# Moving column differences and a residual add to GpSimd, pacing the light work at 0.6, and spacing the scan weights' transfers, in a two-layer image kernel

## The chip, the cores and the metric

The kernel runs on one core of a Trainium2 chip. The metric is the time on the device in microseconds (us): 6881.47 us is the median of three runs (6868.02 to 6881.63). One further execution was taken with the hardware profiler: it took 6861.66 us, and its span from first to last instruction is 6859.9 us. All durations of single instructions come from that execution.

Six actors matter. TensorE (PE) multiplies matrices. VectorE (DVE), ScalarE (ACT) and GpSimd (POOL) do elementwise work. SyncE (SP) only issues transfers (DMA). The DMA engines carry them. Each engine works through its own queue in order: an instruction that waits holds everything behind it on that engine.

## The reference

Four images `x[b]`, each of 96 channels of 128 x 128, pass through two layers with a residual around each. Cut to what matters:

```python
# layer 0: a state-space block on the group-normalised image
z  = silu(dwconv3x3(einsum("bchw,dc->bdhw", gn(x), in_w) + in_b) + dw_b)   # 192 channels
xs = [z by rows, z by columns, both reversed]                              # 4 directions k
dts, B, C = split(einsum("bkdl,ked->bkel", xs, x_proj_weight))
delta = softplus(einsum("bkrl,kdr->bkdl", dts, dt_projs_weight) + bias)    # "scan weights"
h  = scan over l of h = exp(delta * A) * h + delta * B * xs;  y = h * C + Ds * xs
yn = layernorm(sum of the 4 directions) * ln_w + ln_b
x  = x + einsum("bdhw,cd->bchw", yn, out_w) + out_b          # residual of layer 0

# layer 1: on the group-normalised result
xr, x1, x2 = relu_split_norm(gn(x))       # two maps, one for x > 0 and one for x <= 0
key, qry, value = conv3x3(x1, aw1), conv3x3(x2, aw2), conv3x3(x1, aw3)
w_attn = softmax(key patches @ qry patches)                  # a 3x3 kernel per image
y1 = layer_norm(conv3x3(value, w_attn))
y2 = layer_norm(conv3x3(x2, w_conv2)) * x1
x  = x + xr + w_full @ concat(y1, y2) + b_full
```

## The kernel before

The program works in stages, and in most of them two streams of work are woven together. Each stream is a Python generator that emits instructions and yields a cost. `co_run(left, right, pace)` takes a step of `left`, adds its cost times `pace` to a debt, and lets `right` emit until the debt is paid. A larger `pace` therefore lets `right` end sooner beside `left`. The images are numbered 0 to 3.

**Set-up and projection.** `project` makes `z` strip by strip: matmuls on PE (L613), a tanh on ACT (L488), a product on DVE (L489). Beside image 0 it also gathers the statistics of images 1 and 2: `image_stats` loads tiles `xst` from GpSimd's queue (L401), two in flight, and DVE takes their statistics (L404). `other_weights` prepares weights that only the scan and the norm need later. It splits the `dt` weights in three pieces and puts them in place with 54 transfers `wdt` (L246) and 12 transfers `wbc` (L249), all issued by GpSimd. They are emitted in one piece, when the first strips of image 0 have been projected.

**Scan.** `ssm_scan` runs beside the projections of images 1 to 3, beside the norm of image 0, and beside the convolutions of image 0 (`direct_maps`). Each step uses ACT, GpSimd (two products and sums of 128 x 1024, L813 and L846) and DVE (the scan itself, L834).

**Norm.** `Image.norm` is `ssm_output`, then `split_norm`. `ssm_output` works on 16 chunks of 1024 columns. A chunk goes through three rounds of the loop, as `new`, `mid` and `old`. In the last of them `scaled` multiplies the projection by the inverse deviation `r` (L992), adds bias and the residual tile `xr` (L993), and takes statistics (L994), all on DVE and twice for a chunk. The inverse deviations go out to memory and come back spread over the channels, by two transfers on GpSimd's queue (L970, L978); the second waits until the first has landed. `split_norm` has two passes of 16 chunks: the first counts and squares (L1078, L1081, L1085); the second writes the two maps `x1d` and `x2d`. For each chunk and map of the second pass GpSimd clears a column (L1159), ACT scales (L1161), DVE masks (L1166), and SP stores `half`. There are two buffers for each map's `half`.

**Attention of one image.** `attention` has two parts. In the *large convolutions* (`pair_sets`, not for image 0, whose part is `direct_maps`) the weights `wd` convolve `x1d` and `x2d`, and the taps of the softmax are gathered. `Taps.weights` then makes the image's own 3 x 3 weights `wa`. In the *short convolution* these convolve the map `vd`, in 22 chunks of six rows. Both parts use a transform along the columns: `columns` makes from three tiles of rows `y` the tiles `t` that PE multiplies. For the first two tiles there are a difference of 128 x 768 (L1265), a sum (L1266) and a difference (L1267) of 128 x 384; the third is made on DVE (L1272, L1274). The second tile's are always on GpSimd. The first tile's are on the engine `first`: GpSimd in the large convolutions, DVE in the short one. `products` multiplies (L1289, L1300) into four PSUM banks, and `outputs` empties them: ACT copies one (L1338), DVE combines (L1330 to L1333), and DVE takes statistics (L1598 in the short convolution).

**Last stage of one image.** `Image.close` (`attn_output`) mixes the results and writes the output in 16 chunks (L1737 to L1751).

The main loop at the end of the kernel weaves these: beside `attend(b)` runs `close(b - 1)`, and behind it `norm` of image `b + 1`, at a pace of 1.5 for b = 0 and 0.5 afterwards.

```python
        left = imgs[b].attend(psl)
        co_run(left, light, 0.5 if b else 1.5)
        drain(left)
        drain(light)
```

For the part from the set-up to the end of the scan, `in_order` ties each engine's instructions to the order in which they were emitted. After that (from the norm of image 1 on) a scheduler may reorder them.

Of the kernel before, what the change touches and what calls it, by code (L numbers as in the profile page):

```python
# [11 lines left out]
AF = mybir.ActivationFunctionType  # L12
ALU = mybir.AluOpType
# [49 lines left out]
def kernel(  # L63
# [26 lines left out]
    nc = tc.nc  # L90
# [122 lines left out]
    def other_weights():  # L213

        wdt = const.tile([128, 3, NK, 128], BF16, name="wdt", tag="wdt")
        wbc = const.tile([128, 3, 2, 128], BF16, name="wbc", tag="wbc")
        outws = const.tile([C, 2, C], F32, name="outws", tag="outws")  # L220
        outbs = const.tile([C, 1], F32, name="outbs", tag="outbs")
        with (
            tc.tile_pool(name="w0", bufs=1, side="right") as w0,
            tc.tile_pool(name="ps0", bufs=1, space=PSUM, side="right") as ps0,
        ):
            wf = w0.tile([RANK, NK, 2 * C], F32, name="wf")
            nc.gpsimd.dma_start(wf, dt_wT)
            outw = w0.tile([C, 2, C], F32, name="outw")
            nc.sync.dma_start(outw, out_wT)
            one = w0.tile([3, 128], BF16, name="one")  # L230
            nc.vector.memset(one, 1.0)
            nc.vector.memset(wdt, 0.0)
            nc.vector.memset(wbc, 0.0)
            yield
            flat = "p k c -> p (k c)"
            pieces = split3(w0, wf.rearrange(flat), [RANK, NK * 2 * C])
            for row, ch, g, p, n in (
                (row, *part)
                for img, *part in PARTS
                for row in ((KI * img,) if part[1] == 1 else (0, 64))  # L240
            ):
                for w in range(3):
                    src = pieces[w].rearrange("p (k c) -> p k c", k=NK)[:, :, ch : ch + n]
                    for i in range(3):
                        at = row + w * 18 + i * RANK
                        nc.gpsimd.dma_start(wdt[at : at + RANK, g, :, p : p + n], src)  # L246
                for q in range(2):
                    at = row + 54 + q
                    nc.gpsimd.dma_start(wbc[at : at + 5 : 2, g, q, p : p + n], one[:, :n])  # L249
            for j in range(2):  # L250
                nc.vector.tensor_scalar(
                    outws[:, j], outw[:, j], lnw[:, j : j + 1], None, ALU.mult
                )
            pb = ps0.tile([C, 1], F32, name="pb")
            for j in range(2):
                nc.tensor.matmul(
                    pb, lhsT=outw[:, j], rhs=lnb[:, j : j + 1], start=(j == 0), stop=(j == 1)
                )
            nc.vector.tensor_add(outbs, pb, outb)

            pw = ps0.tile([C, C], F32, name="pw")
            for j in range(2):
                nc.tensor.matmul(
                    pw, lhsT=mean192, rhs=outws[:, j], start=(j == 0), stop=(j == 1)
                )
            nc.vector.tensor_sub(outws, outws, pw.unsqueeze(1).to_broadcast([C, 2, C]))
        yield wdt, wbc, outws, outbs
# [647 lines left out]
    def ssm_output(b, yms, xnew, stats, ps, side):  # L915
# [5 lines left out]
        with tc.tile_pool(name="c2", bufs=2, side=side) as p2:  # L921
# [3 lines left out]
            ys, sums_of, near, made = {}, {}, {}, {}  # L925
# [49 lines left out]
            def spread_out(c):  # L975
                xr, to = near[c]
                r = p2.tile([C, SN], F32, name="r")
                nc.gpsimd.dma_start(r, to.partition_broadcast(C))  # L978
                near[c] = xr, r
# [10 lines left out]
            def scaled(c, h, po):  # L990
                xr, r = (t[:, bass.ts(h, CH)] for t in near[c])
                nc.vector.tensor_mul(r, po, r)  # L992
                nc.vector.scalar_tensor_tensor(xr, r, outbs, xr, ALU.add, ALU.add)  # L993
                nc.vector.bn_stats(stats[:, 2 * c + h], xr)  # L994

            for c in range(3):
# [2 lines left out]
            for c in range(NS + 2):  # L999
                new, old = c < NS, c - 2 if c >= 2 else None  # L1000
                mid = c - 1 if 1 <= c <= NS else None
                if old is not None:
                    po = projected(old, 0)
                yield 1.2
                if new:
                    squares(c)
                if mid is not None:
                    inverse(mid)
                    roots(mid)
                if old is not None:  # L1010
                    scaled(old, 0, po)
                    po = projected(old, 1)
                    ys.pop(old)
                if mid is not None:
                    back(mid)
                yield 1.4
                if new:
                    sums(c, 0)
                if mid is not None:
                    spread_out(mid)  # L1020
                yield 1.4
                if old is not None:
                    scaled(old, 1, po)
                    load_y(c + 1)
                if new:
                    sums(c, 1)
                yield 1.4
                if old is not None:
                    nc.sync.dma_start(xnew[:, bass.ts(old, SN)], near.pop(old)[0])
                yield 1.4  # L1030
                if new:
                    rows(c)
                yield 1.4
# [220 lines left out]
    def columns(pool, tiles, r, first):  # L1254

        def of(t, k, p0=0, p1=128):
            v = t[p0:p1, k : k + r * PW].rearrange("p (h w) -> p h w", w=PW)
            return v[:, :, 0:W].rearrange("p h (j e) -> p e h j", e=2)

        made = []  # L1260
        for i, eng in ((0, first), (1, nc.gpsimd)):
            y = tiles[i]
            t = pool.tile([128, 4, CR * W // 2], F32, name=f"t{i}", tag=f"t{i}")
            v = t[:, :, : r * W // 2].rearrange("p i (h j) -> p i h j", h=r)
            eng.tensor_sub(v[:, 0:2], of(y, 0), of(y, 2))  # L1265
            eng.tensor_add(v[:, 2], of(y, 0)[:, 1], of(y, 2)[:, 0])  # L1266
            eng.tensor_sub(v[:, 3], of(y, 2)[:, 0], of(y, 0)[:, 1])  # L1267
            made.append(t)
        y = tiles[2]
        t = pool.tile([128, CR * W // 2], F32, name="t2", tag="t2")  # L1270
        v = t[:, : r * W // 2].rearrange("p (h j) -> p h j", h=r)
        nc.vector.tensor_sub(v[0:64], of(y, 0, 0, 64)[:, 0], of(y, 2, 0, 64)[:, 0])  # L1272
        x = of(y, 0, 64, 128)
        nc.vector.scalar_tensor_tensor(  # L1274
            v[64:128], x[:, 0], signs[64:128], x[:, 1], ALU.mult, ALU.add
        )
        made.append(t)
        return made
# [535 lines left out]
    with tc.tile_pool(name="wp", bufs=1, side="left") as wp:  # L1814
        stats = {}
        stats[0], run = image_stats(0, wp)
        weights = project_weights(wp)
        with tc.tile_pool(name="a0", bufs=8, side="right") as p2:
            drain(run(p2, 8, nc.sync))
        first = len(traced())  # L1820
        others = other_weights()
        for images, pace in (([0], 0.25), ([1], 0.75), ([2, 3], 1.35)):
            left = projections(images, weights, stats, wp, psl)
            if images[0] == 0:
                next(left)
                next(others)
                made = pair_weights()
                next(made)
                while ready[0] < 2:
                    next(left)  # L1830
                maps = [
                    [new_map(f"{n}{i}") for n in ("x1d", "x2d", "vd")] for i in range(2)
                ]
                four, nine = next(made)
                wdt, wbc, outws, outbs = next(others)
            co_run(left, last, pace)
            drain(left)
    istats = [ctx.enter_context(tc.tile_pool(name="istats0", bufs=1, side="left"))]
    imgs = {0: Image(0)}
    left = imgs[0].norm(yms[0][0], psl, "left")  # L1840
    co_run(left, last, 0.5)
    drain(left)
    left = direct_maps(imgs[0], psl)
# [22 lines left out]
    for b in range(NB):  # L1866
        light = []
        if b:
            light.append(imgs[b - 1].close(psr, "right"))
        if b + 1 == 1:  # L1870
            light.append(next_norm)
        elif b + 1 < NB:
            imgs[b + 1] = Image(b + 1)
            light.append(imgs[b + 1].norm(yms[(b + 1) // 2][(b + 1) % 2], psr, "right"))
        light = chain(*light)
        left = imgs[b].attend(psl)
        co_run(left, light, 0.5 if b else 1.5)
        drain(left)
        drain(light)
    drain(imgs[NB - 1].close(psr, "right"))  # L1880
# [75 lines left out]
```

## Time and profile before

| part of the profiled execution | from, us | to, us | length, us |
|---|---|---|---|
| projections (PE, L613) | 49.9 | 2079.2 | 2029.3 |
| norm of image 0, up to its last map | 2131.3 | 2530.8 | 399.5 |
| `direct_maps` of image 0 | 2545.0 | 3567.2 | 1022.2 |
| short convolution of image 0 | 3618.4 | 3816.3 | 197.9 |
| large convolutions of image 1 | 3829.7 | 4598.2 | 768.5 |
| short convolution of image 1 | 4626.6 | 4866.5 | 239.9 |
| large convolutions of image 2 | 4884.3 | 5659.3 | 775.0 |
| short convolution of image 2 | 5687.3 | 5924.6 | 237.3 |
| large convolutions of image 3 | 5943.9 | 6549.3 | 605.4 |
| short convolution of image 3 | 6577.6 | 6736.0 | 158.4 |
| last stage of image 3 | 6750.2 | 6854.6 | 104.4 |

The rows are the times of the first and last matmuls of each part (of the mask L1166 for the norm). A busy share over the whole span (PE 82%, DVE 74%, GpSimd 51%, ACT 42%) averages over parts with different limits, so each part is read on its own. In the views below, a row of the table of stretches gives the window, its length, and for each engine the busy time with the number of instructions in brackets, then the granted clock of PE, the share of the DMA engines in use and the rate in GB/s. A row of the table of waits gives the waiting engine and line, what it waited for, the total in us, how many times, and the longest. A row of the timeline gives start, duration, engine, line, operation, tiles and shapes; a bracket at its end is the idle time ahead of it and what ended it.

### The profile page before, as it was taken

How to read it: one execution, taken by the hardware profiler on the slowest of the kernel's cores; microseconds unless marked ns; L12 is line 12 of the kernel's file. 1: busy time of each engine (PE TensorE's matmuls, PEld its weight loads, DVE VectorE, ACT ScalarE, POOL GpSimd, SP SyncE). 2: the span in 40 equal slices, each digit the busy share in tenths (PEclk: the TensorE clock that was granted, in tenths of full speed). 3: DMA queues.
4: the chain of work that ended last, by engine and by line, in shares of the span. 5: the costliest groups of instructions: out<-in, count | busy, mean ns of one | idle time of the engine just before them, and what ended most of it. 6: DMA issues, size and time to landing. Idle time of an engine off the chain costs nothing. (4 is left out here: it accounts for less than half of the span.)

```text
span 6859.9 us, 74337 instructions
## 1 busy us (share of the span) xinstructions
PE 5650.5 (82%) x22236; PEld 2322.2 (34%) x22236; DVE 5060.8 (74%) x6916; ACT 2912.9 (42%) x3685; POOL 3478.8 (51%) x2264
## 2 busy tenths in 40 slices
PE   5889978978886539899977898887798886788987
PEld 2333323322221114444432343343343342334432
DVE  3247779979897779898458767678766778775688
ACT  1257768777875567676241122132112132121112
POOL 2236759879794339788104434334433434444641
PEclk9999989989996659999988899998899998899998
DMA  6666777866766676766767666567565667565556
GB/s 167 151 160 182 193 214 200 229 165 179 219 176 182 182 205 191 216 174 194 195 186 216 167 166 155 155 170 216 157 176 147 163 163 203 163 173 138 140 155 178
DMA packets 796460, 1227.58 MB, mean 179 GB/s; under 512 B 218750, under 2 KB 558726, under 8 KB 783580
## 3 DMA queue, kind: packets, MB, share of 16 engines
q1 hardware_dynamic: 778572, 1183.90, 63.4%
q0 software_dynamic: 16208, 38.42, 2.0%
q8 instruction: 178, 2.92, 0.2%
q14 instruction: 222, 1.82, 0.1%
q10 hardware_dynamic: 1280, 0.53, 0.0%
HBM read 858.12 MB, written 296.46 MB: 168 GB/s over the span
## 5 line engine op out<-in xcount | busy, mean ns | idle before, releaser
L613 PE MATMUL bank<-y,wp 128*128 128x512 f32 (+3 forms) x3584 | 1317.0, 626 | 94.2 <-DVE z L489 38.6
L1289 PE MATMUL bank<-t,wd 128*128 128x384 f32 (+2 forms) x4224 | 1145.5, 496 | 78.3 <-DVE s L1331 20.6
L1265 POOL TENSOR_TENSOR t<-y 128x768 f32<-128x768 f32 (+1 forms) x352 | 565.4, 1607 | 1257.2 <-PE bank L1289 391.4
L846 POOL TENSOR_TENSOR y<-y,dl 128x1024 f32<-128x1024 f32 x384 | 1051.4, 2738 | 258.6 <-DVE dl L838 228.3
L813 POOL TENSOR_TENSOR dl<-dl,u 128x1024 f32<-128x1024 f32 x384 | 1004.4, 2616 | 249.7 <-ACT dA L789 122.4
L834 DVE TENSOR_TENSOR_SCAN dA<-dA,pBC 128x512 f32<-128x512 f32 x768 | 981.4, 1278 | 30.9
L1338 ACT COPY s<-bank 128x384 f32<-128x384 f32 (+2 forms) x292 | 135.9, 465 | 1900.0 <-PE bank L1300 1837.5
L1289 PEld LDWEIGHTS bank<-t,wd 128*128 128x128 f32 (+1 forms) x4224 | 557.2, 170 | 622.0 <-issue 323.4
L727 PE MATMUL pBC<-xr,wbc 60*128 60x512 bf16 (+1 forms) x1536 | 459.9, 403 | 349.6 <-DVE dA L834 276.2
L838 DVE TENSOR_TENSOR dl<-dA,pBC 128x512 f32<-128x512 f32 x768 | 528.1, 688 | 272.3 <-PE pBC L727 199.8
L1289 PE MATMUL bank<-t,wa 128*96 128x384 f32 (+1 forms) x1408 | 561.3, 548 | 202.8 <-DVE t L1266 128.7
L613 PEld LDWEIGHTS bank<-y,wp 128*128 128x128 f32 (+3 forms) x3584 | 459.1, 169 | 764.9 <-issue 661.2
L1647 PE MATMUL bank<-y,wn 128*128 128x384 f32 (+5 forms) x2408 | 670.2, 505 | 38.4 <-ACT ring L1661 16.1
L656 ACT ACTIVATE dl<-pd,dtb 128x512 f32<-128x512 f32 x768 | 486.3, 684 | 172.0 <-PE pd L727 163.8
L817 DVE TENSOR_TENSOR pBC<-dl,pBC 128x512 f32<-128x512 f32 x768 | 527.5, 687 | 4.7 <-POOL dl L813 3.8
L1330 DVE TENSOR_TENSOR d<-s,bank 128x384 f32<-128x384 f32 (+2 forms) x292 | 155.8, 534 | 486.1 <-ACT s L1338 435.8
L789 ACT ACTIVATE dA<-dl,negA 128x1024 f32<-128x1024 f32 x384 | 420.3, 1141 | 2.3
L1647 PEld LDWEIGHTS bank<-y,wn 128*128 128x128 f32 (+3 forms) x2408 | 306.2, 167 | 335.2 <-issue 165.9
L1289 PEld LDWEIGHTS bank<-t,wa 128*96 128x96 f32 x1408 | 241.0, 184 | 507.9 <-issue 305.6
L1266 POOL TENSOR_TENSOR t<-y 128x384 f32<-128x384 f32 (+1 forms) x352 | 382.2, 1086 | 0.0
L727 PEld LDWEIGHTS <-wbc 60*128 60x128 bf16 (+1 forms) x1536 | 103.5, 96 | 781.7 <-issue 767.6
L656 ACT ACT_TABLE_LOAD x245 | 314.3, 1283 | 109.0 <-PE pd L727 102.3
(257 smaller groups left out, 7965.0 us busy)
## 6 DMA issues: line engine op xcount, KB each, us to landing
u<-zb SPq DMA_DIRECT2D x192, 1024.0 KB
yms<-y SPq DMA_DIRECT2D x96, 512.0 KB
y<-yms SPq DMA_DIRECT2D x64, 768.0 KB
xn<-xnew SPq DMA_DIRECT2D x128, 384.0 KB
y<-y SPq DMA_DIRECT2D x128, 258.2 KB
zb<-z SPq DMA_DIRECT2D x64, 512.0 KB
y<-vd SPq DMA_DIRECT2D x168, 193.8 KB
y<-in_x SPq DMA_DIRECT2D x56, 480.0 KB
```

What stands on the lines that cost most here:

```text
L613: nc.tensor.matmul(blocks(pz[p:e]), lhsT=ws[k][:, d, c : c + e - p], rhs=window(ys[k], at, d, n), start=(i == 0), stop=(i == len(terms) - 1),)
L656: nc.scalar.activation(dst, src, AF.Softplus, bias=bias)
L727: nc.tensor.matmul(p, lhsT=w[rows], rhs=xr[rows, at : at + CH], start=True, stop=True)
L789: nc.scalar.activation(live[m]["dA"], live[m]["dl"], AF.Exp, scale=negA[:, g % 3, k : k + 1])
L813: nc.gpsimd.tensor_mul(t, t, u_view(n))
L817: nc.vector.tensor_mul(p, live[n]["dl"][:, bass.ts(half, CH)], p)
L834: nc.vector.tensor_tensor_scan(h, h, p, init, ALU.mult, ALU.add)
L838: nc.vector.tensor_mul(live[n]["dl"][:, sl], live[n]["dA"][:, sl], live[n]["C", half])
L846: nc.gpsimd.tensor_add(v, v, t.rearrange("p (a b) -> p a b", b=W))
L1265: eng.tensor_sub(v[:, 0:2], of(y, 0), of(y, 2))
L1289: nc.tensor.matmul(pc[p:e, :n], lhsT=w[:, i, c : c + e - p], rhs=t[k][:, i, :n], start=(k == 0), stop=False,)
L1647: nc.tensor.matmul(pc[p:e, :n].rearrange("p (h w) -> p h w", w=W), lhsT=w[:, c : c + e - p], rhs=v[:, :, 0:W], start=(i == 0), stop=(i == ...
```

## The change

```diff
@@ other_weights @@
                 for w in range(3):
+                    yield
                     src = pieces[w].rearrange("p (k c) -> p k c", k=NK)[:, :, ch : ch + n]
...
@@ main part, after pair_weights @@
-                wdt, wbc, outws, outbs = next(others)
+                got = next(others)
+                while not got:
+                    next(left)
+                    got = next(others)
+                wdt, wbc, outws, outbs = got
...
@@ ssm_output: scaled @@
                 nc.vector.tensor_mul(r, po, r)
-                nc.vector.scalar_tensor_tensor(xr, r, outbs, xr, ALU.add, ALU.add)
+                nc.gpsimd.tensor_add(xr, r, xr)
                 nc.vector.bn_stats(stats[:, 2 * c + h], xr)
...
                 if mid is not None:
+                    xr = near[mid][0]
+                    nc.scalar.activation(xr, xr, AF.Identity, bias=outbs)
                     spread_out(mid)
...
@@ columns @@
             eng.tensor_sub(v[:, 0:2], of(y, 0), of(y, 2))
-            eng.tensor_add(v[:, 2], of(y, 0)[:, 1], of(y, 2)[:, 0])
-            eng.tensor_sub(v[:, 3], of(y, 2)[:, 0], of(y, 0)[:, 1])
+            nc.gpsimd.tensor_add(v[:, 2], of(y, 0)[:, 1], of(y, 2)[:, 0])
+            nc.gpsimd.tensor_sub(v[:, 3], of(y, 2)[:, 0], of(y, 0)[:, 1])
...
@@ main loop @@
-        co_run(left, light, 0.5 if b else 1.5)
+        co_run(left, light, 0.6 if b else 1.5)
```

Four things change.

- **Scan weights.** The 54 `wdt` transfers come in 18 groups of three. Between two groups one step of the projection is emitted.
- **Residual.** The bias goes into the loaded residual tile on ACT, one instruction of 96 x 1024 for a chunk. The sum of 96 x 512 moves from DVE to GpSimd, twice for a chunk. The statistics stay on DVE and now read what GpSimd wrote.
- **Columns.** In the short convolution, the sum and the small difference of the first tile move from DVE to GpSimd. In the large convolutions they were there already.
- **Pace.** Beside the attention of images 1 to 3, the light work is emitted at a pace of 0.6 instead of 0.5.

## The prediction on record

> **What bounds the kernel now.** The chain that ended last covers only the final stage, so I read the table of stretches first, cut at the borders of the parts.
>
> ```profile
> 4160.00:4558.00 398.00, 361.00 (x1712) 162.99 (x1709) 283.38 (x403) 72.83 (x118) 159.87 (x173) 0.94 0.60 160
> ...
> 4627.00:4884.00 257.00, 192.82 (x550) 80.68 (x549) 213.72 (x316) 50.02 (x61) 109.49 (x93) 0.81 0.71 200
> ...
> 6577.00:6736.00 159.00, 145.54 (x526) 61.68 (x528) 144.03 (x222) 11.00 (x23) 77.33 (x57) 0.98 0.60 168
> ```
>
> The first row is the large convolutions of image 1 beside the norm: PE is busy 361 of 398 us (91%), DVE 71%. The second is the short convolution of image 1 beside the norm's second pass, the third that of image 3 with nothing beside it. The same work takes 240 us there and 158 us here; alone it fills PE and DVE alike (146 and 144 of 159 us). Next, the waits in the short convolution of image 1:
>
> ```profile
> POOL t L1265 <- DMA y<-vd: 69.8, 16, 8.1
> ...
> PE bank L1289 <- DVE t L1266: 52.5, 15, 4.5
> ```
>
> PE waits 15 times for the first tile, which DVE makes from behind the masks of the second pass. PE's granted clock falls to 0.81 there, so its matmuls stretch as well (193 us busy against 146). Third, the timelines of GpSimd, DVE and PE around the scan weights:
>
> ```profile
> 183.84 4.95 POOL L246 DMA_DIRECT2D wdt<-piece  x9
> 188.78 1.08 POOL L249 DMA_DIRECT2D wbc<-one  x2
> 189.85 1.07 POOL L401 DMA_DIRECT2D xst<-in_x  x2
> ```
>
> ```profile
> 192.78 0.69 DVE L404 BATCH_NORM_STATS2 stats<-xst 96x6 f32<-96x512 f32 x1 [40.94 <-DMA xst<-in_x]
> ```
>
> ```profile
> 194.11 7.66 PE L613 MATMUL bank<-y,wp 128*64 128x512 f32 x28 [31.17 <-DVE z L489]
> ```
>
> The tile `xst` is queued on GpSimd behind all the weights' transfers. DVE stands 40.9 us in front of it, the product `z` is behind it on DVE, and PE stands 31.2 us. Fourth, the residual in image 0's norm (DVE, then GpSimd):
>
> ```profile
> 2203.09 0.62 DVE L992 TENSOR_TENSOR r<-bank,r 96x512 f32<-96x512 f32 x1
> 2203.74 0.75 DVE L993 SCALAR_TENSOR_TENSOR xr<-r,outbs,xr 96x512 f32<-96x512 f32 x1
> 2204.53 0.69 DVE L994 BATCH_NORM_STATS2 xstats<-xr 96x6 f32<-96x512 f32 x1
> ```
>
> ```profile
> 2203.46 0.55 POOL L970 DMA_DIRECT2D rd<-mq  x1 [3.96 <-DVE mq L968]
> 2205.54 0.52 POOL L978 DMA_DIRECT2D r<-rd  x1 [1.53 <-DMA rd<-mq]
> 2206.07 2.37 POOL L813 TENSOR_TENSOR dl<-dl,u 128x1024 f32<-128x1024 f32 x1
> ```
>
> DVE does it back to back, while GpSimd is held by a transfer that waits for another.
>
> **What the Trainium skill says.** "GPSIMD Engine Reference", section 3.1, gives an fp32 add of 2048 elements as 4497 ns on GpSimd and 2293 on DVE, 1.96 times. Here the sum L1266 averages 1086 ns on GpSimd and 968 on DVE; both means hold interference, and the measured ones are used. Section 8 of that page says that the two share SBUF interfaces and contend when DVE reads two SBUF inputs. The trace agrees: beside GpSimd's columns one residual (L993) took 6689 ns, where the median is 747. "DMA: Bandwidth & Descriptors", section on the anatomy of one DMA, puts about 2 us of fixed cost on a transfer, mostly completion; the 1.53 us hold at L978 fits. "Perfetto Trace Analysis", on the most-contended engine, calls matmul busy time a bad measure; the 193 against 146 us for the same matmuls agrees, so I compare lengths of parts.
>
> **The change part by part**, against the span of 6859.9 us.
>
> *Scan weights.* The transfers stay: 54 x 560 + 12 x 546 ns = 36.8 us of GpSimd. In the changed program's order, single `xst` loads now stand between groups of 3 to 11 of them, and one load more stands ahead. Behind the gap DVE takes one `xst` every 5.8 us (203.88, 209.70 in the timeline); nine such steps are 52 us, room for 36.8 + 9 x 0.51 = 41.4 us of issues. A group of 11 holds a load by 6 us, and with two buffers a load has about 11.6 us. So nearly all of PE's 31.2 us goes; I leave 4 for the first group: **-27** (-31 to -10). The projection is one chain on PE here and the scan has not begun, so it passes to the end. The added projection steps come before `co_run` starts and only shift emission: 0.
>
> *Pace.* In the changed order on DVE, all 32 masks of the norm stand ahead of the short convolution's first evacuation, 14 of them ahead of the softmax's maximum and 18 behind; in the kernel before most stood between the short convolution's chunks. So the short convolutions of images 1 and 2 should take image 3's time: (239.9 - 158.4) + (237.3 - 158.4) = **-160** (-162 to -130). The masks must go somewhere. Behind the softmax's maximum there are 9 pairs. In image 0, where they also stand together, SP's stores of `x1d` begin at 3572.11, 3577.28, 3582.64 and 3588.58: 5.5 us a pair, since two buffers wait for the stores. 9 x 5.5 = 49 us to the first evacuation, where image 1 now has 25 (maximum 4609.2, evacuation after the first products, 4634.5): +24 for each image, **+48** (+10 to +80). Ahead of the maximum, 7 pairs at 5.5 are 38 us beside some 55 us of large convolution, in which DVE gets 55 x 0.59 (its share alone in image 3) + 14 x 1.58 = 55 us, so full: I take 10 us for each image, **+20** (0 to +60). The loads of rows for PE are behind these stores on SP, which waits for the masks; that is in the upper bound. The rest of the light work only moves closer together; PE has the same work at the same 91%: 0.
>
> *Columns.* 88 sums and 88 differences leave DVE (85.2 + 81.2 us) for GpSimd, 22 chunks for each image. GpSimd then has per chunk 1.69 + 4 x 1.23 = 6.6 us in image 3 (its own rows there), DVE 144 - 34 = 110 us of 159. PE works 6.6 us a chunk and has 7.2. GpSimd is a chunk ahead and also waits for `vd`, so it just fits: image 3 0 (-8 to +15), and images 1 and 2 are priced by it above. In image 0, whose masks stay in the short convolution, PE waited 27 us for L1266, but GpSimd also sits there behind column clears that wait for stores (37 us): **-10** (-25 to 0).
>
> *Residual.* DVE loses 128 x 1.17 = 149 us, off the path where PE is at 91%. ACT gains 64 instructions, 1.24 us each by L1161 (same shape, same operation), with ACT 18% busy: hidden, and the residual's load has been issued well before. GpSimd gains 128 adds of 1.2 us (half of L813's 2.37; bounds 0.8 to 2.7): hidden by 60% idle time in the large convolutions. But the statistics now wait for GpSimd. In image 0 the order is as written: the first half costs 1.2 instead of 0.75, the second is behind the spread transfer: from the end of L992 at 2203.71 to 2206.06 + 1.2 is 3.5 us instead of 0.8. That is 3.2 us for each chunk, and up to 2.4 more with a scan product in front. Behind those statistics stand the reciprocal and the scan. DVE waits 39 us there for `mq` and `r` (2.4 a chunk), which will take up most: 16 x 1 = **+15** (-5 to +50). In the norms of images 1 to 3 the scheduler puts other DVE work (some 8 us by its rows) between product and statistics: 0 (-10 to +130).
>
> Sum: -27 - 160 + 48 + 20 - 10 + 15 = -114, a span of 6746, -1.66%. The unprofiled median is 6881.47: 6881.5 x 0.9834 = **6767**.
>
> **The rivals.** *(A) More.* The masks cost nothing in the large convolutions and the gap: -160 - 27 - 10 = -197, that is 6684. For it: DMA is at 0.60 there. Against it: 5.5 us a pair was measured.
>
> *(B) Only moved.* The second pass costs the large convolutions what it cost the short ones, 80 us an image instead of 34: -114 + 92 = -22, 6859. For it: the pairs in a row are bound by their stores. Against it: most of the 80 us was a tangle of DVE's order and GpSimd's clears, which goes.
>
> *(C) Slower: the statistics' wait takes DVE.* An add stands behind a group of columns on GpSimd (1.45 + 0.84 + 0.82 = 3.1 us) and behind the spread transfer; DVE stops at the statistics, the evacuations behind it stop, PE runs out of banks. If each chunk loses 3.1 + 2.4 = 5.5 us in images 0, 2 and 3 that is 48 x 5.5 = 264 us: -114 - 15 + 264 = +135, 7017. It decides from 129 / 48 = 2.7 us a chunk. For it: in the stretch of the first row GpSimd waits 114.7 us for DVE's `mq` and 54.1 us for PE. Against it: the order leaves 8 us.
>
> That the change doesn't do what it says is excluded by the order of its instructions.
>
> **Chances.** Forecast 0.55, A 0.15, B 0.16, C 0.14. Its own bounds added in squares are about 50 us each way (6717 to 6817); the range reaches up to B and a mild C, and down towards A: 6700 to 6885. About 0.2% (14 us) is what a measurement tells from no change. Faster: 0.55 + 0.15 + most of B (0.11) = 0.81; same 0.04; slower 0.15.
>
> **What would show it.** Right: PE's 31 us gap at 160 gone; short convolutions of images 1 and 2 at 155 to 165 us with PE waiting little for `t`; the gap behind the softmax some 24 us longer; statistics' waits on GpSimd near 3 us a chunk in image 0, near none later. Wrong: short convolutions above 190 us with PE waiting for GpSimd's `t`; large convolutions above 830 us; DVE idle ahead of the statistics by over 130 us in all.

## The result and the profile after

The changed kernel takes 6773.61 us (median of four runs, 6767.27 to 6776.06) against 6881.55 us for the kernel before (four runs). The ratio is **0.9846**, interval 0.9829 to 0.9864: 108 us or 1.5% faster. The forecast was 6767 us. In the profiled execution the span went from 6859.9 to 6772.8 us, 87 us less.

By the medians the total came out near the forecast, but partly by luck. Beside the later run of the same code the kernel before took 6864.5 us and the changed one 6771.6, 93 us less (ratio 0.9862, interval 0.9844 to 0.9879, which leaves the forecast's 0.9834 just outside), and the two profiles are 87 and 89 us shorter than that of before, where the prediction's sum was 114. This table sets the terms of the prediction's sum against the two profiles taken of the changed kernel (the second belongs to a later run of the same code and shows how far such lengths repeat). All figures are differences to the profile of before, in us, from the first and last matmuls of each part; the ends of gaps are those of the neighbouring parts. A gap is the stretch between the last matmul of the large convolutions and the first of the short one. Rows of a few us (the last stage of image 3 among them) are left out, so the second sum differs from its span by 3.

| part | predicted | changed kernel | again |
|---|---|---|---|
| set-up and projections | -27 | -23 | -28 |
| norm of image 0, its 16 output projections | +15 | +18 | +18 |
| from there to the end of `direct_maps` | 0 | +3 | +9 |
| short convolution of image 0 | -10 | -11 | -14 |
| short convolutions of images 1 and 2 | -160 | -176 | -176 |
| gaps ahead of these two | +48 | +59 | +58 |
| large convolutions of images 1 and 2 | +20 | +42 | +40 |
| large convolutions of image 3 | 0 | +17 | +17 |
| gap and short convolution of image 3 | 0 | -16 | -16 |
| sum | -114 | -87 | -92 |

First the table of stretches after (length, then busy time and instructions of PE, PEld, DVE, ACT and GpSimd, granted clock, DMA share, GB/s): the large convolutions and the short convolution of image 1, and the short convolution of image 3.

```profile
3819.00:4616.00 797.00, 685.12 (x3099) 318.98 (x3097) 512.34 (x761) 213.61 (x309) 347.06 (x335) 0.92 0.62 165
4673.90:4824.60 150.70, 150.05 (x528) 63.85 (x528) 126.83 (x191) 14.27 (x26) 106.51 (x97) 0.99 0.73 207
...
6503.40:6647.90 144.50, 142.44 (x528) 62.47 (x528) 117.90 (x184) 11.34 (x23) 109.64 (x95) 0.99 0.66 184
```

The short convolution of image 1 went from 240 to 151 us. PE is busy for all of it, at a granted clock of 0.99 instead of 0.81, and DVE has only 127 us of work there, instead of 214 in the 257 us of the prediction's row. For the large convolutions, the row of the whole part in the kernel before is this:

```profile
3829.70:4598.20 768.50, 684.24 (x3090) 312.70 (x3094) 526.89 (x742) 170.33 (x259) 294.86 (x295) 0.94 0.62 163
```

PE has the same work (685 and 684 us) and the part is 28 us longer: what was packed in there beside it was not free (ACT, for one, was busy 214 us instead of 170). The waits around the short convolution of image 1 after (window 4600 to 4690):

```profile
PE bank L1293 <- DMA wa<-watd: 41.1, 1, 41.1
POOL half L1163 <- DMA x1d<-half: 30.7, 7, 12.2
```

The 15 waits of PE for the first tile (52.5 us before) are gone. Ahead of the part there is now one wait of 41.1 us, for the weights `wa`. GpSimd meanwhile waits 30.7 us, and ACT 20.1, for buffers of the masked maps, whose stores are under way.

The set-up after, DVE and then PE:

```profile
185.49 0.69 DVE L406 BATCH_NORM_STATS2 stats<-xst 96x6 f32<-96x512 f32 x1 [6.58 <-DMA xst<-in_x]
```

```profile
168.79 7.93 PE L615 MATMUL bank<-y,wp 128*64 128x512 f32 x28 [10.42 <-DVE z L491]
```

DVE's one wait of 40.9 us for `xst` has become several, of which this one, 6.6 us, is the longest. PE's 31.2 us in front of the projection have become 10.4. What is left is another wait: the product `z` that PE waits for stood 14.3 us for ACT's `z` on DVE, not for `xst`; in the kernel before no such wait was over 4.9 us.

Last, DVE's waits in the norm of image 0 (window 2110 to 2355):

```profile
DVE xstats L996 <- POOL xr L995: 99.2, 30, 9.7
DVE mq L960 <- DMA mq<-st: 15.2, 3, 13.1
```

The statistics wait 30 times for GpSimd's sum, 3.3 us each time, which is 6.2 us for each of the 16 chunks. For comparison the kernel before had waits for `r` and `mq` (window 2131 to 2358):

```profile
DVE r L992 <- DMA r<-rd: 19.0, 6, 5.0
DVE mq L958 <- DMA mq<-st: 15.5, 6, 6.3
```

### The profile page after: what moved, and what is told of

Read it like the earlier page. It is cut to its first block, busy times and chain, and to the rows that moved or that the text cites. A ratio compares the mean times of both kernels' runs of the same rounds, so it can differ in the third digit from the quotient of the medians.

```text
span 6772.8 us, 74661 instructions
## 1 busy us (share of the span) xinstructions
PE 5600.1 (83%) x22236; PEld 2315.3 (34%) x22236; DVE 4783.9 (71%) x6612; ACT 2984.4 (44%) x3749; POOL 3789.6 (56%) x2568
## 3 DMA queue, kind: packets, MB, share of 16 engines
q14 instruction: 224, 1.84, 0.1%
## 5 line engine op out<-in xcount | busy, mean ns | idle before, releaser
L1293 PE MATMUL bank<-t,wd 128*128 128x384 f32 (+2 forms) x4224 | 1162.7, 503 | 62.1 <-ACT s L1342 21.6
L1293 PEld LDWEIGHTS bank<-t,wd 128*128 128x128 f32 (+1 forms) x4224 | 575.2, 173 | 602.1 <-issue 340.7
L1293 PE MATMUL bank<-t,wa 128*96 128x384 f32 (+1 forms) x1408 | 496.8, 500 | 148.1 <-DMA wa<-watd 125.2
L1270 POOL TENSOR_TENSOR t<-y 128x384 f32<-128x384 f32 (+1 forms) x440 | 454.1, 1032 | 127.7 <-DMA y<-vd 82.8
L1271 POOL TENSOR_TENSOR t<-y 128x384 f32<-128x384 f32 (+1 forms) x440 | 432.7, 984 | 0.0
L1293 PEld LDWEIGHTS bank<-t,wa 128*96 128x96 f32 x1408 | 220.5, 168 | 415.0 <-issue 228.6
```

What stands on the lines that cost most here:

```text
L1270: nc.gpsimd.tensor_add(v[:, 2], of(y, 0)[:, 1], of(y, 2)[:, 0])
L1293: nc.tensor.matmul(pc[p:e, :n], lhsT=w[:, i, c : c + e - p], rhs=t[k][:, i, :n], start=(k == 0), stop=False,)
```

## The experiments

The theory at this point was the prediction's: four edits, each worth its term. The rivals were that the gains come from another edit than the one I credited, that a gain is given back later, or that the residual costs more (rival C) or less than its term. All ratios below are to the kernel before, run beside the kernel in question.

### One edit alone, four times

**Scan weights alone.** The edit is the first two pieces of the diff.

```diff
                 for w in range(3):
+                    yield
...
-                wdt, wbc, outws, outbs = next(others)
+                got = next(others)
+                while not got:
+                    next(left)
+                    got = next(others)
```

> The kernel before with the scan weights' transfers spread out alone. My theory: PE's gap of 31 us in the projection of image 0 shrinks to under 10, and the 23 to 27 us gained there reach the end: ratio 0.9960 to 0.9967. Rival (given back): the stretch up to the end of direct_maps is bound by the scan, which does not start earlier, so the end of direct_maps stays at 3567 us and the ratio is within 0.9985 to 1.0015.

Measured: 0.9956 (0.9941 to 0.9970), span 6833.0 us, 27 less than before. The projections end at 2051.9 instead of 2079.2 us and `direct_maps` at 3541.8 instead of 3567.2. Two waits of PE for `z` are left in the set-up, 11.1 us together, as in the changed kernel (11.0). What is won in front of the scan is still there at its end and at the end of the program, so it was not given back.

**Columns alone.**

```diff
-            eng.tensor_add(v[:, 2], of(y, 0)[:, 1], of(y, 2)[:, 0])
-            eng.tensor_sub(v[:, 3], of(y, 2)[:, 0], of(y, 0)[:, 1])
+            nc.gpsimd.tensor_add(v[:, 2], of(y, 0)[:, 1], of(y, 2)[:, 0])
+            nc.gpsimd.tensor_sub(v[:, 3], of(y, 2)[:, 0], of(y, 0)[:, 1])
```

> The kernel before with the two column operations on GpSimd alone; the norm's second pass still lies beside the short convolutions of images 1 and 2. My theory: 10 us less in image 0; in images 1 and 2 the wait of PE for the first tile (52 and 49 us) mostly goes, since GpSimd makes it without standing behind the masks, so the short convolutions fall from 240 to about 200 us: in all 70 to 100 us less, ratio 0.985 to 0.990. Rival (tangle): those waits pass to GpSimd's column clears and to vd's loads behind the stores of the maps, the short convolutions stay above 230 us, and the ratio is 0.996 to 1.000.

Measured: **0.9826** (0.9808 to 0.9844), the largest of the four and more than I expected; the medians differ by 122 us, the spans by 126. The short convolution of image 1, its row of the table of stretches, and its waits:

```profile
4614.50:4809.60 195.10, 163.47 (x529) 68.12 (x529) 181.09 (x248) 47.48 (x57) 133.06 (x123) 0.92 0.84 241
```

```profile
PE bank L1300 <- DVE t L1274: 29.1, 14, 3.4
```

It takes 195 us instead of 240 (image 2: 197 instead of 238), with the masks still beside it (ACT's and DVE's instruction counts show them: 57 and 248 against 26 and 191 in the changed kernel). PE no longer waits for the first tile; it waits 29 us for the third, which DVE makes. The gap ahead is 25 us and the large convolutions have not grown. Images 0 and 3, beside whose short convolutions the pace changes nothing, give 14 us each. Half of what I had credited to the pace comes from the columns alone, and without its price.

**Residual alone.**

```diff
-                nc.vector.scalar_tensor_tensor(xr, r, outbs, xr, ALU.add, ALU.add)
+                nc.gpsimd.tensor_add(xr, r, xr)
...
+                    xr = near[mid][0]
+                    nc.scalar.activation(xr, xr, AF.Identity, bias=outbs)
```

> The kernel before with the residual's sum on GpSimd and the bias on ACT alone. My theory: 15 to 20 us more in the norm of image 0, where DVE's statistics stand waiting for GpSimd, and nothing in the other images: ratio 1.0022 to 1.0030. Rival C (the statistics' wait takes DVE in all norms): 130 us or more, ratio above 1.015. Rival (relief): the 149 us taken from DVE shorten the large convolutions of images 1 and 2, ratio below 0.998.

Measured: 1.0043 (1.0028 to 1.0057), a loss of 27 us by the medians and 30 by the ratio, about twice the term. DVE's waits in the norm of image 0 of this kernel:

```profile
DVE xstats L994 <- POOL xr L993: 96.5, 30, 9.1
```

This is the wait of the changed kernel, 3.2 us each time, and the part is 18 us longer. `direct_maps`, beside which the norm of image 1 runs with the same wait (51.1 us, 30 times, by its table of waits), is 14 us longer. Two profiles of one kernel differ by up to 7 us in that part, so all fourteen profiles of this document have to be taken together. The norm of image 0 lasts 244 to 245 us in the six profiles that have the residual's sum on GpSimd with the statistics right behind it, and 220 to 227 in the seven that have it on DVE: 22 us more by the means. `direct_maps` lasts 1026 to 1036 us in the seven profiles with the sum on GpSimd and 1022 to 1030 in the other seven: 7 us more. The two places together are the size of the loss. Rival C asked for 264 us; nothing of that size is there.

**Pace alone.**

```diff
-        co_run(left, light, 0.5 if b else 1.5)
+        co_run(left, light, 0.6 if b else 1.5)
```

> The kernel before with the pace of 0.6 alone. My theory: the short convolutions of images 1 and 2 fall from 240 and 237 us to 158, as image 3's, 160 us less; the gap behind the softmax and the last part of the large convolutions take 70 to 100 us of it back: 60 to 92 us less in all, ratio 0.9866 to 0.9913. Rival (columns did it): without the columns on GpSimd the short convolutions stay above 200 us and the ratio is above 0.996.

Measured: 0.9952 (0.9939 to 0.9964), span 26 us less. The short convolution of image 1:

```profile
4692.90:4852.70 159.80, 152.43 (x528) 63.42 (x528) 148.86 (x229) 14.29 (x26) 77.75 (x59) 0.98 0.69 195
```

It does become as short as image 3's, 160 us, and image 2's too: 158 us won, as the prediction said. But the gaps grow by 58 us, the large convolutions of images 1 and 2 by 65 and those of image 3 by 15. Of the 158 us, 138 go back, where I had expected 70 to 100.

### Two edits on the same wait

**The changed kernel without the residual,** then **without the columns.** Each puts the lines of the kernel before back at that place.

> The changed kernel with the residual's sum back on DVE in one instruction. Theory 1 (the residual costs what it cost alone, in the norm of image 0 and beside direct_maps): about 20 to 35 us less than the changed kernel, ratio to the kernel before 0.980 to 0.982. Theory 2 (with the norm packed closer at 0.6, relief of DVE in the large convolutions pays for it): no gain, ratio 0.984 to 0.986.

Measured: 0.9832 (0.9814 to 0.9849), span 6747.9 us, 25 less than with the residual; the medians differ by 20 to 22 us. That lies between the two theories. The residual is likely a loss in this company too (the intervals of the two ratios overlap), somewhat smaller than alone.

> The changed kernel with the short convolution's two column operations back on DVE. Theory 1 (pace and columns overlap: either of them clears the short convolutions of images 1 and 2): it loses what the columns bring when no mask is beside them, 9 us for each of images 1 and 2, 14 for image 3, 11 for image 0, about 43 us: ratio 0.990 to 0.992. Theory 2 (their gains add): it loses 126 us, ratio 1.001 to 1.004.

Measured: 0.9925 (0.9909 to 0.9941). Against the changed kernel (0.9846, and 0.9862 in the run below) the columns are worth 0.6 to 0.8% beside the pace, where they are worth 1.74% alone. Four edits alone add up to -0.44 - 1.74 + 0.43 - 0.48 = -2.2%; together they give -1.4 to -1.5%. The missing part is what columns and pace both take from the same place, the short convolutions of images 1 and 2: 86 and 158 us alone, but 176 together.

**Scan weights and columns without pace and residual.**

> The kernel before with the scan weights and the columns alone: neither residual nor pace. Theory 1 (with the columns on GpSimd, the pace of 0.6 takes more from the large convolutions and the gap than it gives, and the residual is a loss): 150 to 155 us less than before, ratio 0.977 to 0.979, ahead of the changed kernel by some 45 us. Theory 2 (pace is needed): ratio 0.984 or more.

Measured: **0.9784** (0.9769 to 0.9800), median 6726.1 us, faster than the changed kernel. The kernel without the residual, which ran with it, differs from it by the pace alone: 0.9832 against 0.9784. So with the columns in place, a pace of 0.6 is not a gain but a loss of 0.4 to 0.5% (25 us between the medians, and the intervals do not overlap). By the parts of the two profiles it takes 99 us from the short convolutions of images 1 and 2 and adds 60 to the gaps and 59 to the large convolutions.

**The changed kernel once more,** beside the runs with a third buffer and with later statistics:

> The changed kernel itself, unedited, as the measure for the three beside it: 0.983 to 0.986 of the kernel before.

Measured: 0.9862 (0.9844 to 0.9879), median 6771.59 us, in agreement with the first measurement. Its parts are in the table at the top.

### Where the gap comes from

In the gap ahead of the short convolution of image 1 in the changed kernel, the timelines of SP (SPq is its queue), of DVE and of PE:

```profile
4644.10 0.37 SPq L1174 DMA_DIRECT2D x1d<-half  x1
...
4662.85 0.37 SPq L1174 DMA_DIRECT2D x1d<-half  x1
...
4663.74 1.41 SPq L1467 DMA_DIRECT2D watd<-ring  x1
...
4670.29 0.30 SPq L1235 DMA_DIRECT2D wa<-watd  x1
```

```profile
4636.80 0.82 DVE L1198 SCALAR_TENSOR_TENSOR ring<-ring 96x288 f32<-96x288 f32 x2
```

```profile
4631.08 1.68 PE L1462 MATMUL bank<-ident,sm 96*96 96x96 f32 x9 [4.76 <-DVE sm L1456]
4673.86 7.34 PE L1293 MATMUL bank<-t,wa 128*96 128x384 f32 x16 [41.10 <-DMA wa<-watd]
```

And in the kernel before, DVE and SP at the same place:

```profile
4618.85 0.82 DVE L1194 SCALAR_TENSOR_TENSOR ring<-ring 96x288 f32<-96x288 f32 x2
```

```profile
4619.70 0.30 SPq L1463 DMA_DIRECT2D watd<-ring  x1
```

PE has transposed the softmax at 4632.8 us, and DVE has made the weights from it at 4637.6, 21 us behind the last large convolution, as in the kernel before. There their way to memory (`watd`, L1463) is issued at once. Here it is issued only at 4663.74, 26 us later, because SP works in order and 33 other transfers stand ahead of it: 16 loads of rows `y` for the short convolution, 5 stores of the large convolutions' results, and, of the norm's second pass, 4 loads `xn` and 8 stores of masked maps. Just ahead SP has stood 9.1 us for a mask, whose buffer the next `xn` needs. In these 26 us it hardly waits (3.3 us, 1.1 of them for masks): issuing the 33 takes it 22 us. Between 4644.10 and 4662.85 three more pairs of masked maps went out, one every 6.3 us. Two experiments act on this.

**The weights' store and loads on ACT's queue.**

```diff
-            nc.sync.dma_start(watd, wt)
+            nc.scalar.dma_start(watd, wt)
...
-            ws = stacked_weights(p1, img.watd, "wa")
+            ws = stacked_weights(p1, img.watd, "wa", nc.scalar)
```

> The changed kernel with the store of the image's own weights and their loads issued by ACT instead of SP. Theory 1 (the longer gap is these transfers standing on SP behind the stores of the masked maps): the gaps of images 1 and 2 fall from 57 us to 30 to 38, and the kernel gains 30 to 50 us on the changed one, ratio 0.977 to 0.980. Theory 2 (the gap is DVE's nine pairs of masks, which hold the first evacuation anyway): the first matmuls come sooner but wait again, the sum of gap and short convolution stays within 10 us, ratio 0.983 to 0.986.

Measured: 0.9897 (0.9884 to 0.9910), slower than the changed kernel and outside both ranges. The gaps fall from 57 to 31 us, so SP's order was what held PE. But the short convolutions of images 1 and 2 grow from 151 to 183 and 189 us, and image 0's from 187 to 199. The waits of this kernel from 4615 to 4830:

```profile
POOL half L1163 <- DMA x1d<-half: 34.4, 8, 12.6
...
PE bank L1293 <- POOL t L1270: 23.5, 3, 21.7
...
PE bank L1293 <- DMA wa<-watd: 15.2, 1, 15.2
```

The pairs of the second pass now fall into the short convolution again. GpSimd waits for their buffers with its columns behind, and PE waits for those (21.7 us once). Gap and short convolution together are 5 us longer than in the changed kernel for image 1 and 13 for image 2: issuing the weights earlier does not take the pairs away.

**A third buffer for the masked maps,** with the square's scratch cut to one buffer to make room.

```diff
-                z = p2.tile([C, SN], F32, name="xz")
+                z = p2.tile([C, SN], F32, name="xz", bufs=1)
...
-                    h = p2.tile([C, RS, PW], F32, name=f"half{side_}")
+                    h = p2.tile([C, RS, PW], F32, name=f"half{side_}", bufs=3)
```

> The changed kernel with three instead of two buffers for each masked map (and one instead of two for a square that nobody reads). Theory 1 (the nine pairs behind the softmax go at the pace of two buffers waiting for their stores, and the weights' transfers on SP stand behind them): a third buffer takes a third of each wait, the gaps of images 1 and 2 fall from 57 to 42 to 50 us, 15 to 30 us in all. Theory 2 (the rate is set elsewhere: by SP's order or by the DMA engines): the gaps stay within 4 us of 57 and the time within 10 us.

Measured: 0.9803 (0.9783 to 0.9823), 42 us below the changed kernel run with it. The waits around the gap, from some 16 us ahead of it to 16 us behind it, with three buffers (window 4571.6 to 4653) and in the changed kernel beside it (4593.1 to 4682):

```profile
PE bank L1293 <- DMA wa<-watd: 34.2, 1, 34.2
...
POOL half L1163 <- DMA x1d<-half: 24.7, 6, 6.0
```

```profile
PE bank L1293 <- DMA wa<-watd: 39.8, 1, 39.8
POOL half L1163 <- DMA x1d<-half: 28.2, 6, 12.5
```

GpSimd's waits for a buffer are little shorter in sum but half as long at most, ACT's fall from 26.0 to 5.7 us, SP has 22 transfers ahead of the weights instead of 33 and holds them 17.6 us instead of 24.8, and the two gaps are 49 and 48 us instead of 56 and 57. So the two buffers do set part of the gap, but only 16 us lie there. By the two profiles, which differ by 48 us, the rest lies in the other places where the second pass or its stores run: image 0's second pass (-7), its short convolution (-8) and the large convolutions of three images (-17, no more than these lengths scatter). What the smaller scratch does by itself was not tried.

**The same third buffer on scan weights and columns.**

> Scan weights and columns alone, with the same third buffer. Theory 1 (with the masks beside the short convolutions, GpSimd's clears and SP's stores still hold the columns' loads): the short convolutions of images 1 and 2 fall from about 200 to 180 to 190 us, 20 to 40 us in all, ratio 0.973 to 0.976. Theory 2 (the DMA engines, 0.84 in use there, are the limit): nothing, ratio 0.977 to 0.980.

Measured: **0.9734** (0.9716 to 0.9752), median 6683.84 us: the fastest of all, ahead of both kernels. The ratio falls in the range of Theory 1, but by luck, since my place for the gain was wrong: the short convolutions of images 1 and 2 stay at 201 and 192 us (203 and 198 with two buffers). By the profiles the gain is in the large convolutions (757 and 757 us against 783 and 769) and in image 0's second pass (81 against 89). The profile with two buffers is 22 us longer than the median of its kernel, so how much of the 26 us in the large convolutions of image 1 is the buffer's stays open.

### How much of the residual's loss is the wait

**Statistics taken one half later.** They are emitted behind the product and the sum of the next half.

```diff
                 nc.gpsimd.tensor_add(xr, r, xr)
-                nc.vector.bn_stats(stats[:, 2 * c + h], xr)
+                while behind:
+                    behind.pop()()
+                behind.append(lambda: nc.vector.bn_stats(stats[:, 2 * c + h], xr))
```

> The changed kernel with each statistics instruction of the norm emitted behind the next half's product and sum, so that GpSimd has done its sum by then; the residual stays on GpSimd and its bias on ACT. Theory 1 (in the norm of image 0 the loss is DVE standing in front of its statistics): DVE's wait for GpSimd there falls from 99 to under 25 us, the projections of that norm take 220 to 230 us instead of 245, and the kernel gains 12 to 25 us on the changed one. Theory 2 (the loss comes from the bias on ACT and from GpSimd's sums ahead of the scan's products): the wait falls but the length stays above 238 us, and nothing is gained.

Measured: 0.9849 (0.9824 to 0.9875), with the changed kernel at 0.9862 beside it: no difference that the intervals allow. The norm of image 0 is 234 us long, between the two theories, where it is 245 in the changed kernel and 227 before (220 to 227, by the mean 222, in the seven profiles with the sum on DVE). DVE's waits there:

```profile
DVE mq L961 <- DMA mq<-st: 74.2, 13, 12.9
```

The wait for GpSimd's sum is gone from the list altogether, yet the part keeps 7 of its 18 us, or 12 of the 22 by the means. DVE now waits 74.2 us for `mq`, 15.5 before. What stood behind the residual's wait has become the wait: `mq`, the sums of the next chunk, which come over ACT's queue and from matmuls that follow in the same loop. GpSimd meanwhile is held at its own step, the spread transfer, by the table of its waits in this window:

```profile
POOL r L981 <- DMA rd<-mq: 74.7, 15, 7.2
```

In the changed kernel that was 55.3 us (12 times). The wait of the statistics explains about 11 us. What costs the rest was not tried; ACT, which has got the bias and is busy 135 us in this norm instead of 116, is a candidate.

## Why the prediction was right, and where it was wrong

**Scan weights: right.** -27 predicted, -23 and -28 in the two profiles, -27 for the edit alone. The step "nearly all of PE's 31.2 us goes" held to two thirds in place (10.4 us are left, which now wait for ACT and not for `xst`); the end of the projections lies between 2076.9 and 2083.3 us in the kernels without the edit, so the remaining few us are within what this end scatters. That it "passes to the end" is shown by the end of `direct_maps` in the run with this edit alone.

**Pace, the short convolutions: right in size, wrong in author.** 158 us with the pace alone against 160 predicted. But the step that priced the columns in images 1 and 2 inside the pace's term hid that the columns alone take 86 us from the same two parts (45 + 41). They ended PE's wait for the first tile, for which the prediction quoted 52.5 us, in the plainest way: the tile no longer stands on DVE behind the masks. The prediction also put PE's longer matmuls there (193 us busy against 146) down to the granted clock. By the ratio of the clocks, 0.98 to 0.81, the 146 us would be 177, so the clock is at most a part; the row's 24 further matmuls are another.

**Pace, the gaps: right in size, by another path.** +48 predicted, +59 measured. The pairs' stores come every 6.3 us there, where 5.5 was taken. But the prediction had PE stop at the first evacuation, which DVE makes behind the pairs. PE stops earlier, for its weights, which SP holds 26 us behind 33 other transfers; of SP's order the prediction named only that the loads of rows stand behind the stores, as part of the upper bound. The 31 us gaps with the other queue show that path. With the weights out of the way the pairs cost as much in the short convolution, so their price was the right thing to estimate.

**Pace, "the rest of the light work only moves closer together; PE has the same work at the same 91%: 0": this step failed.** The large convolutions of images 1 and 2 grew by 42 us, not 20, and those of image 3, which the sum leaves out, by 17. There the last stage of image 2 runs alone beside PE, with neither norm nor masks. That the pace does it holds through all runs: the parts of images 1 and 2 together are 1576 to 1610 us in the eight profiles at 0.6 and 1514 to 1552 in the six at 0.5. The term that was priced, the masks in the last 55 us, was nearly right: the last tenth of the matmuls takes 61.5 and 62.8 us in images 1 and 2, where it took 49.1 and 49.2, so 13 us each and not 10. What was put at nothing is the rest, 16 us in images 1 and 2 by these two profiles and 17 in image 3 (3 to 7 in the other kernels at 0.5, 6 to 17 in those at 0.6). Waits of PE on DVE in the large convolutions of image 1, after and before:

```profile
PE bank L1754 <- DVE c L1743: 21.4, 10, 4.5
PE bank L1388 <- DVE ring L1337: 15.8, 3, 11.8
PE bank L1388 <- DVE s L1335: 13.7, 9, 7.9
```

```profile
PE bank L1750 <- DVE c L1739: 16.3, 8, 3.4
PE bank L1384 <- DVE ring L1333: 11.5, 2, 6.8
...
PE bank L1384 <- DVE s L1331: 6.6, 5, 3.1
```

These three groups rise from 34.4 to 50.9 us; the one wait of 11.8 us lies in the last tenth, beside the masks. Not every wait grew: one of 8.7 us for DVE's `o` is gone. But all waits of PE in this part rise from 84 to 112 us, which is the 28 us, and from 58 to 73 in number: those for DVE by 13 us, for ACT by 10, for GpSimd by 4.5. So a PE at 91% had small waits in it, and light work that comes closer together made more of them and made them longer. What the second pass costs in gap and large convolutions is (59 + 42) / 2 = 50 us an image, and 61 with the pace alone: between the forecast's 34 and rival B's 80.

**Columns: image 0 right (-10, measured -11 and -14); image 3 wrong.** The step "so it just fits: image 3 0" gave nothing where 14 us were won. GpSimd's 6.6 us a chunk was too high, and DVE's load, not PE's, had been what held the part above PE's 145 us: PE waited 11.2 us for DVE's `s` in the kernel before and waits 0.3 us after. GpSimd's instructions in image 3, by form, after and then before:

```profile
L1271 POOL TENSOR_TENSOR t<-y 128x384 f32<-128x384 f32 x36 | 38.6, 1071 | 0.0
L1270 POOL TENSOR_TENSOR t<-y 128x384 f32<-128x384 f32 x36 | 37.3, 1036 | 34.3 <-issue 22.6 <-DMA y<-vd 7.3 <-POOL t L1271 3.0
L1269 POOL TENSOR_TENSOR t<-y 128x768 f32<-128x768 f32 x18 | 33.1, 1840 | 3.5 <-DMA y<-vd 3.4
```

```profile
L1265 POOL TENSOR_TENSOR t<-y 128x768 f32<-128x768 f32 x18 | 31.6, 1753 | 89.7 <-PE bank L1289 54.4 <-DMA y<-vd 32.9 <-issue 2.4
L1266 POOL TENSOR_TENSOR t<-y 128x384 f32<-128x384 f32 x18 | 22.0, 1221 | 0.0
```

A sum fell from 1221 to 1036 ns as DVE's own sums left. A chunk costs GpSimd 1.84 + 2 x 1.04 + 2 x 1.07 = 6.1 us, and PE 144.5 / 22 = 6.6: PE is the bound, at 142 of 144.5 us.

**Residual: right in image 0 (+15, measured +18), the whole too small.** The working there gave waits of 1.2 and 3.5 us for the two halves of a chunk and up to 2.4 more; 6.2 us were measured, within that, though above the "near 3 us a chunk" that was named as the sign of being right. The cost stayed small as argued: DVE's other waits there fell from 40 to 16 us and its work from 181 to 126. Alone, the edit costs 27 to 30 us. The step that failed is "in the norms of images 1 to 3: 0", for image 1 beside `direct_maps`, where the profiles show 7 us. In the changed kernel DVE waits 48 us for GpSimd's sums in that norm, and 24 in each of the next two, where "near none" was expected. On the other side it takes work from DVE in the large convolutions: those of images 1 and 2 together are 11 us shorter with it than without (1587 against 1598), no more than these lengths scatter.

**The rivals.** A falls: the masks do cost the gap and the large convolutions. B as a whole falls (6859 against 6773), though the pass costs more in its new place than the forecast had. C's mechanism is there, at 18 us over 16 chunks, 1.1 us a chunk (1.4 by the means), well below the 2.7 from which it decides.

So the forecast's total held in part because two errors met: the pace was priced some 50 us too cheap (11 in the gaps, 22 and 17 in the large convolutions), and the short convolutions gave 32 us that were not in the sum (16 in images 1 and 2, 16 in image 3 with its gap). With some 9 us in the smaller terms this leaves the profile 27 us short of the sum.

## What to carry to other kernels

When two edits remove the same wait, price each of them alone and then on top of the other: here the columns alone gave 1.74%, and the pace, a gain of 0.5% by itself, became a loss of 0.4 to 0.5% beside them. Work taken from a full stage and packed into one where PE is at 91% is not free; ask which of PE's small waits there ends on the engine that gets the work. Where a transfer that PE waits for shares an issuing queue with the moved work, count what will stand ahead of it: here 33 transfers and 26 us. And before a producer moves to another engine, look at what stands behind its consumer in that engine's queue.

## What the runs showed of the hardware

**Two-input sums on DVE beside GpSimd.** In the kernel before, 117 of the 128 residual sums on DVE (L993, two inputs in SBUF) took 0.73 to 0.84 us. The other 11 took 3.3 to 10.2 us, 54 us more than the usual 0.75 in all. The longest one, and the last of GpSimd's sums and differences beside it:

```profile
5552.82 10.24 DVE L993 SCALAR_TENSOR_TENSOR xr<-r,outbs,xr 96x512 f32<-96x512 f32 x1
```

```profile
5561.69 0.82 POOL L1267 TENSOR_TENSOR t<-y 128x384 f32<-128x384 f32 x1
```

GpSimd ran ten such operations back to back during these 10.24 us, none longer than the mean of its kind, and then paused. All 11 held sums ended 0.55 to 0.56 us behind GpSimd's last operation of such a run, and in each case GpSimd then did not start anything for at least 6 us. Of the 117 others only one ran beside GpSimd's sums or products for more than 0.3 us. So in this kernel the held sum was let through when GpSimd paused, and not slowed in proportion. The statistics of the same tiles (L994, one input) never took more than 0.69 us. In the other direction GpSimd's sums of 128 x 384 in the short convolution of image 3 became 15% faster (1221 to 1036 ns) when as many of DVE's had gone to GpSimd, but its differences of 128 x 768 became 5% slower (1753 to 1840 ns). The held sums and the faster ones fit "GPSIMD Engine Reference" in the Trainium skill, section 8, by which the two engines contend over shared SBUF interfaces when DVE reads two SBUF inputs; that the changed lengths on GpSimd come from this, and not from other traffic in the stretch, was not tried on its own.

**Issuing takes time too.** In the gap SP needed 22.0 us to issue 33 transfers, 0.3 to 1.7 us each, while its waits came to 3.3 us.

**A third buffer** mattered less there than the pairs' steady distance suggested: around the gap GpSimd's waits for a buffer of `x1d` fell from 28.2 to 24.7 us, and PE's wait for `wa` from 39.8 to 34.2.
